# An adaLN transformer block on one core: the modulation is made with the conditions as TensorE's stationary side and turned back, and the condition is loaded and activated ahead of the biases

## The chip, the cores and the metric

The kernel runs on one core of a Trainium2 chip. The metric is device time in microseconds for one execution, the median of several. Five engines work side by side, each with its own queue in program order: TensorE (PE, with its weight loads shown apart as PEld), VectorE (DVE), ScalarE (ACT), GpSimd (POOL) and SyncE (SP), which here only issues DMAs. ScalarE issues some DMAs too, in line with its other instructions.

## The reference

Sixteen batches of 224 tokens of width 512, a condition vector of 512 per batch, and a context of 750 tokens per batch. Everything is float32.

```python
c_proj = jax.nn.silu(c) @ W_mod + b_mod
shift_a, scale_a, gate_a, shift_m, scale_m, gate_m = jnp.split(c_proj, 6, axis=-1)
x_norm = modulate(_ln(x), shift_a, scale_a)        # t * (1 + scale) + shift, per batch
q, k, v = split(x_norm @ W_qkv + b_qkv)            # 16 heads of 32
x = x + gate_a[:, None] * (attention(q, k, v) @ W_proj + b_proj)
x = x + cross_attention(_ln(x), _ln(context)) @ W_cproj + b_cproj
x_norm2 = modulate(_ln(x), shift_m, scale_m)
h = jax.nn.gelu(x_norm2 @ W_mlp1 + b_mlp1)
x = x + gate_m[:, None] * (h @ W_mlp2 + b_mlp2)
```

The change touches only how the first two lines are made. The condition is 16 x 512, W_mod is 512 x 3072. The six parts of 512 columns are numbered 0 to 5: shift, scale, gate of self-attention, then shift, scale, gate of the MLP.

## The kernel before

The kernel has three stages one after the other: self-attention in 8 pairs of batches (`p`), cross-attention in 16 batches, and the MLP in 7 groups of 512 tokens. `Ordered` makes every engine keep the order in which the program issues, so each engine's queue is as written.

The head (lines 248 to 274 and 589 to 608) loads the condition, the parts of W_mod and the first two batches; activates the condition (`c_act`), turns it so that its 512 features lie on partitions (`c_t`); turns all biases, which are loaded as rows of 128 (`brow`), to columns (`bcol`), and adds 1 to those of the scales; norms the first two batches (`norms[j].all()`: bn_stats on DVE, the rest on POOL); and calls `make_part(0)` and `make_part(1)`. Then `turn_x` turns the normed rows on PE, and DVE applies shift and scale while it evicts them to `xt`, from which q, k and v are projected.

A shift or scale is wanted as columns: `mod_t` holds, for each 128 features, one column per batch. `make_part` therefore takes 128 x 128 blocks of W_mod as the stationary side and the 16 columns of `c_t` as the moving one: 16 matmuls, each streaming 16 columns. In the profile one float32 matmul of this kind is two rows of PE. A gate (parts 2 and 5) is wanted as rows: there `c_t` is stationary (16 columns) and W_mod streams 512 columns, in 4 matmuls; the bias rows `bg` are added and the gate is written to DRAM, from where it is read back spread over the token rows.

Parts 0 and 1 are made in the head. The other four are placed in the first units of self-attention. A unit is one group of 4 heads in one batch; `plan[p, u, slot]` lists what else runs in the two slots of unit `u` of pair `p`. Part 2 is at (0, 1, 0), part 3 at (0, 1, 1), parts 4 and 5 at (0, 3, 0) and (0, 3, 1). The loads of W_mod go through two buffers, so a later part's load waits until PE has used the buffer. All small PE results pass through `ps_mm`, three PSUM banks in rotation, and a bank is free again when it has been evicted. One unit on PE is: scores, slot 0, the weights of the unit before (`weights_t`), the turn of the row maxima, slot 1, the values and sums of the unit before.

The DMAs of SP and ScalarE take turns on a small set of completion semaphores. A DMA can thus wait, at its issue, for an unrelated earlier one that used the same semaphore; this decides some of the waits at the head.

Of the kernel before, what the change touches and what calls it, by code (L numbers as in the profile page):

```python
# [8 lines left out]
F32 = mybir.dt.float32  # L9
BF16 = mybir.dt.bfloat16  # L10
AF = mybir.ActivationFunctionType
ALU = mybir.AluOpType
# [25 lines left out]
def kernel(  # L38
# [23 lines left out]
    nc = Ordered(tc)  # L62
    B, N, H = x.shape
    S = context.shape[1]
    MLP = w_mlp1.shape[1]
    P = 128
    NH = 16
    HD = H // NH
    KC = H // P
# [20 lines left out]
    SCALE = float(HD) ** -0.5  # L90
# [3 lines left out]
    const = ctx.enter_context(tc.tile_pool(name="const", bufs=1))  # L94
# [3 lines left out]
    ident = const.tile([P, P], F32, name="ident")  # L98
# [33 lines left out]
    o_mod, o_qkv = 0, 6 * KC  # L132
    o_qc = o_qkv + 3 * KC
    o_kvc = o_qc + KC
    o_mlp = o_kvc + 2 * KC
    nbias = o_mlp + NF
    brow = const.tile([nbias, P], F32, name="brow")
    for off, vec in ((o_mod, b_mod), (o_qkv, b_qkv), (o_qc, b_qc), (o_kvc, b_kvc), (o_mlp, b_mlp1)):
        rows = vec.shape[0] // P
        nc.scalar.dma_start(out=brow[off : off + rows, :], in_=vec.rearrange("(r p) -> r p", p=P))  # L140
    bcol = const.tile([P, nbias], F32, name="bcol")

    def bias_rows(pool, vec, rows, name):
# [21 lines left out]
    def load_w(pool, w, name, bufs=1):  # L165
        kc = w.shape[0] // P
        t = pool.tile([P, kc, w.shape[1]], F32, name=name, bufs=bufs)
        nc.sync.dma_start(out=t, in_=w.rearrange("(k p) n -> p k n", p=P))
        return t

    mm, turn = nc.tensor.matmul, nc.tensor.transpose
# [65 lines left out]
    mp = mod_pool.enter_context(tc.tile_pool(name="mod", bufs=2, side="right"))  # L237
    attention_psum = ExitStack()
    ps_s = attention_psum.enter_context(tc.tile_pool(name="at_s", bufs=1, space=PSUM))
    ps_mm = attention_psum.enter_context(tc.tile_pool(name="at_mm", bufs=3, space=PSUM))  # L240
    ps_o = attention_psum.enter_context(tc.tile_pool(name="at_o", bufs=1, space=PSUM))
    xs = {}
    w_part = {}

    def load_part(i):
        w_part[i] = load_w(mp, w_mod[:, i * H : (i + 1) * H], "w_mod", 2)

    c_in = mp.tile([B, H], F32, name="c_in", bufs=1)
# [3 lines left out]
        xs[b] = load_x(sa, tokens(x, b), 6)  # L252
    load_part(1)
    wq, wk, wv = (load_w(ws, w_qkv[:, i * H : (i + 1) * H], f"wqkv{i}") for i in range(3))
    bg = mp.tile([B, 2, H], F32, name="bg", bufs=1)
    for i in range(2):
        lo = (2 + 3 * i) * H
        nc.scalar.dma_start(out=bg[:, i, :], in_=b_mod[lo : lo + H].partition_broadcast(B))

    c_act = mp.tile([B, H], F32, name="c_act", bufs=1)  # L260
    nc.scalar.activation(c_act, c_in, AF.Silu)

    c_t = mp.tile([P, KC, B], F32, name="c_t", bufs=1)
    ps = ps_mm.tile([P, 512], F32, name="mm")
# [1 line left out]
        turn(ps[:, k * B : (k + 1) * B], c_act[:, k * P : (k + 1) * P], ident[:B, :B])  # L266
    nc.vector.tensor_copy(c_t.rearrange("p k b -> p (k b)"), ps[:, : KC * B])

    ps = ps_mm.tile([P, 512], F32, name="mm")
    turn(ps[:, :nbias], brow, ident[:nbias, :nbias])  # L270
    nc.vector.tensor_copy(bcol, ps[:, :nbias])
    for i in (1, 4):
        sl = bcol[:, o_mod + i * KC : o_mod + (i + 1) * KC]
        nc.vector.tensor_scalar(sl, sl, 1.0, None, ALU.add)

    bqc = const.tile([P, KC], F32, name="bqc")
    nc.vector.tensor_scalar(bqc, bcol[:, o_qc : o_qc + KC], SCALE, None, ALU.mult)

    def make_part(i):
        w = w_part[i]  # L280
        ps = ps_mm.tile([P, 512], F32, name="mm")
        if i % 3 == 2:
            for k in range(KC):
                mm(ps[:B, :H], c_t[:, k, :], w[:, k, :], start=(k == 0), stop=(k == KC - 1))
            g = mp.tile([B, H], F32, name="gates", bufs=1)
            nc.vector.tensor_tensor(g, ps[:B, :H], bg[:, i // 3, :], ALU.add)
            nc.sync.dma_start(out=gate_d[i // 3], in_=g)
        else:
            slot = (i // 3) * 2 + i % 3
            for m in range(KC):  # L290
                for k in range(KC):
                    mm(
                        ps[:, m * B : (m + 1) * B], w[:, k, m * P : (m + 1) * P], c_t[:, k, :],
                        start=(k == 0), stop=(k == KC - 1),
                    )
            for m in range(KC):
                nc.vector.tensor_scalar(
                    mod_t[:, slot * KC + m, :], ps[:, m * B : (m + 1) * B],
                    bcol[:, o_mod + i * KC + m : o_mod + i * KC + m + 1], None, ALU.add,
                )  # L300
# [99 lines left out]
    def whole(products):  # L400
        for _ in products:
            pass
# [32 lines left out]
    if True:  # L435
# [8 lines left out]
        def project_qk(p, m):  # L444
            ps = ps_mm.tile([P, 512], F32, name="mm")
            for k in range(KC):
                mm(
                    ps[:, :PN], (wq, wk)[m // KC][:, k, (m % KC) * P : (m % KC + 1) * P], xts[p][k],
                    start=(k == 0), stop=(k == KC - 1),
                )  # L450
                if k == 1:
                    yield
            t = sa.tile([P, PN], F32, name="qk", bufs=6)
            bm = bcol[:, o_qkv + m : o_qkv + m + 1]
            if m < KC:
                nc.vector.tensor_scalar(t, ps[:, :PN], bm, SCALE, ALU.add, ALU.mult)
            else:
                nc.scalar.activation(t, ps[:, :PN], AF.Identity, bias=bm)
            qk[p, m] = t
# [30 lines left out]
        def project(p, t):  # L490
            b, c = PB * p + t // TC, t % TC
            if c == 0:
                gate[b] = gate_rows(sa, 0, b * N, TP)
            ps = ps_mm.tile([P, 512], F32, name="mm")
            yield from project_heads(ps, at[p], wproj, t * TP)
            add_to_x(sa, ps[:TP, :H], xs[b][:, c, :], bproj, gate[b])
            if c == TC - 1:
                nc.sync.dma_start(out=x_self[b], in_=xs[b])
# [3 lines left out]
        def at_slot(p, u, slot, f):  # L502
            if p < NP:
                plan.setdefault((p, u, slot), []).append(f)

        for p in range(NP):
            if p < NP - 1:
                for g in range(1, KC):
                    at_slot(p, 2 * g - 2, 0, lambda p=p, g=g: whole(project_qk(p, g)))
                    at_slot(p, 2 * g - 2, 1, lambda p=p, g=g: whole(project_qk(p, KC + g)))  # L510
                for t in range(PT if p else 0):
                    at_slot(p, 1 + t // 2 * 2, t % 2, lambda p=p, t=t: whole(project(p - 1, t)))
            else:

                left = [(project_qk, p, m) for m in (1, KC + 1, 2, KC + 2)]
                left += [(project, p - 1, t) for t in range(2)]
                left += [(project_qk, p, m) for m in (3, KC + 3)]
                left += [(project, p - 1, t) for t in range(2, PT)]
                parts = [h for f, *args in left for h in halves(lambda f=f, args=args: f(*args))]
                for i, h in enumerate(parts):  # L520
                    at_slot(p, i // 3, i % 3 // 2, h)
            if p == 0:
                at_slot(p, 1, 0, lambda: make_part(2))
                at_slot(p, 1, 1, lambda: make_part(3))
                at_slot(p, 1, 1, lambda: load_part(4))
                at_slot(p, 1, 1, lambda: load_part(5))
                at_slot(p, 3, 0, lambda: make_part(4))
                at_slot(p, 3, 1, lambda: make_part(5))
                at_slot(p, 3, 1, load_cross)
            n = p + 1  # L530
            if n < NP:
                if n > 1:
                    at_slot(p, 0, 0, lambda n=n: fetch(n))
                at_slot(p, 1, 0, lambda n=n: norm_begin(n))
                for t in range(PT):
                    at_slot(
                        p, 1 + t // 2, t % 2, lambda n=n, t=t: norms[PB * n + t // TC].stats(t % TC)
                    )
                for j in range(PB):
                    at_slot(p, 1 + j, 1, lambda n=n, j=j: norms[PB * n + j].apply())  # L540
                for k in range(KC):
                    at_slot(p, 4, k // 2, lambda n=n, k=k: turn_x(n, k))
                for t in range(PT):
                    at_slot(p, 5 + t // 2, t % 2, lambda n=n, t=t: project_v(n, t))
                at_slot(p, 7, 0, lambda n=n: whole(project_qk(n, 0)))
                at_slot(p, 7, 1, lambda n=n: whole(project_qk(n, KC)))
# [42 lines left out]
        norm_begin(0)  # L589
        for j in range(PB):  # L590
            norms[j].all()
        make_part(0)
        make_part(1)
        load_part(2)
        load_part(3)
        fetch(1)
# [142 lines left out]
    class First:  # L739
# [22 lines left out]
        def part(self):  # L762
            return cw["mx"].tile([P, H], F32, name="mx")
# [39 lines left out]
    with tc.tile_pool(name="ca", bufs=2, reuse_waits="tile") as ca:  # L803
# [98 lines left out]
        for b in range(B):  # L902
            n = b + 1
            for g in range(KC):
                f, m = (b, g + 1) if g < KC - 1 else (n, 0)
# [399 lines left out]
```

## Time and profile before

| what | value |
| --- | --- |
| runs shown | 2964.05, 2967.8, 2962.16 us; median 2964.05 |
| profiled execution | 2967.63 us |
| its span, first to last instruction | 2965.8 us |
| what lies around the span | 1.83 us |
| mean granted TensorE clock | 0.989 |
| PE rows / busy | 19901 / 2877.7 us |
| first matmul | 9.97 us |
| first normed tile `xt` | 25.57 us |
| scores of unit 4 end | 98.9 us |

All times of the trace are microseconds from the start of the span. In a timeline row the first number is the start, the second how long the piece lasts (several merged instructions may be one piece), then engine, line, operation, out<-in, the shape, the count, and in brackets the idle time before it and what ended that. Nearly all instructions show line 28, the recording helper of `Ordered`, so they are told apart by tile names. A line of the windows gives the stretch, its length, busy time and count of PE, PEld, DVE, ACT and POOL, and last the granted clock, the DMA share and GB/s. A busy PE is not PE at its peak: ends of matmuls are modelled.

### The profile page before, as it was taken

Reading aid. Unit: us, or ns where it says so; the run is one execution under the profiler, and the core shown is the slowest. Engines: PE = TensorE matmul, PEld = TensorE weight load, DVE = VectorE, ACT = ScalarE, POOL = GpSimd, SP = SyncE. Lnnn points to the kernel's source line nnn. Section 1 sums busy time; section 2 is a strip of 40 time slices with the busy share of each in tenths; the row PEclk is TensorE's granted clock in tenths of the full one; section 3 lists DMA queues with packets and bytes.
Section 4 is the critical chain, followed back from the end, with each engine's and each line's share of the span. In section 5 each row is a group of like instructions: output and inputs, shape, how many; then the busy total and the mean of one; then the engine's idle time right before and its main releaser. Section 6 shows DMA issues by size and latency. Waiting matters only on the chain.

```text
span 2965.8 us, 47584 instructions
## 1 busy us (share of the span) xinstructions
PE 2877.7 (97%) x19901; PEld 1851.1 (62%) x19901; DVE 1843.2 (62%) x2624; ACT 1175.4 (40%) x1462; POOL 1289.0 (43%) x1636
## 2 busy tenths in 40 slices
PE   8999999999999999999999999999988999999999
PEld 5544444544455655555556556555655888888888
DVE  2556555566377777777777877877776633443343
ACT  1122121222356656656665666566553122112211
POOL 1022211122266766766767766667664510221021
PEclk9999999999999999999999999999999999999999
DMA  5111101100100101000011001010011211111110
GB/s 183 63 32 32 32 10 29 53 20 20 60 21 22 34 24 34 30 19 31 24 34 34 24 22 34 24 34 24 7 58 67 74 36 54 43 40 36 54 43 29
DMA packets 55387, 114.47 MB, mean 39 GB/s; under 512 B 4308, under 2 KB 4372, under 8 KB 55172
## 3 DMA queue, kind: packets, MB, share of 16 engines
q1 hardware_dynamic: 54560, 110.58, 11.6%
q8 instruction: 156, 2.56, 0.4%
q10 hardware_dynamic: 612, 0.85, 0.1%
q14 instruction: 59, 0.48, 0.1%
HBM read 89.33 MB, written 22.09 MB: 38 GB/s over the span
## 4 chain that ended last, share of the span: by engine, by line
PE 81%; DVE 7%; issue 4%; ACT 3%; POOL 3%; DMA 1%; SPq 0%; ACTq 0%; POOLq 0%; DVEq 0%
PE mm L28 46%; PE a L28 10%; PE sc L28 9%; PE o L28 9%; PE b L28 5%; ACT pt L28 3%; PE c L28 3%; DVE top L28 1%; POOL acc L28 1%; DVE rinv L28 1%; DVE stats L28 1%; DVE mc L28 1%; DVE m L28 1%; ACT kt L28 1%; POOL upd L28 0%
## 5 line engine op out<-in xcount | busy, mean ns | idle before, releaser
L28 POOL TENSOR_TENSOR acc<-acc,pt 125x448 f32<-125x448 f32 x512 | 585.1, 1143 | 40.2
L28 DVE TENSOR_TENSOR pt<-pt,o 125x896 f32<-125x896 f32 x384 | 394.3, 1082 | 92.1 <-PE o L28 87.0
L28 ACT COPY pt<-sc 125x1792 f32<-125x1792 f32 x192 | 317.5, 1654 | 223.3 <-DVE top L28 198.9
L28 DVE TENSOR_TENSOR top<-top,sc 125x896 f32<-125x896 f32 x320 | 346.6, 1083 | 40.7 <-PE sc L28 34.0
L28 POOL TENSOR_TENSOR upd<-upd,gate 112x512 f32<-112x512 f32 (+1 forms) x60 | 79.1, 1318 | 668.9 <-DVE upd L28 664.3
L28 PE MATMUL mm<-wkvc,cxt 128*125 128x512 f32 x768 | 354.4, 604 | 8.6 <-ACT kt L28 8.6
L28 PE MATMUL mm<-cxt,wkvc 128*128 128x375 f32 x1024 | 349.8, 484 | 2.4 <-ACT cxt L28 2.4
L28 ACT ACTIVATE pt<-pt 125x896 f32<-125x896 f32 x384 | 339.1, 955 | 12.6 <-DVE pt L28 11.9
L28 POOL TENSOR_TENSOR acc<-pt 125x448 f32<-125x448 f32 x128 | 146.6, 1146 | 380.3 <-ACT pt L28 380.3
L28 DVE RECIPROCAL rinv<-o 128x224 f32<-128x224 f32 x128 | 198.7, 1553 | 108.6 <-PE o L28 108.6
L28 PEld LDWEIGHTS mm<-cxt,wkvc 128*128 128x128 f32 x1024 | 190.1, 191 | 112.4 <-issue 12.8
L28 DVE TENSOR_REDUCE m<-sc 112x8 f32<-112x1792 f32 x64 | 129.7, 2026 | 209.4 <-PE sc L28 209.4
L28 ACT ACTIVATE pt<-sc 112x1792 f32<-112x1792 f32 x64 | 106.5, 1665 | 365.4 <-PE sc L28 365.4
L28 PEld LDWEIGHTS mm<-wkvc,cxt 128*125 128x125 f32 x768 | 136.5, 187 | 175.1 <-issue 153.5
L28 POOL TENSOR_TENSOR rstd<-mv,eps 112x2 f32<-112x2 f32 (+3 forms) x93 | 18.0, 194 | 475.7 <-DVE mv L28 475.7
L28 PE MATMUL sc<-qt,kt 32*125 32x224 f32 x3072 | 202.7, 378 | 12.9 <-ACT pt L28 12.3
L28 PE MATMUL mm<-xt,wqkv 128*128 128x448 f32 x512 | 209.6, 552 | 4.7 <-DVE xt L28 4.7
L28 PEld LDWEIGHTS sc<-qt,kt 32*125 32x125 f32 x3072 | 134.0, 184 | 92.9 <-issue 41.2
L28 ACT COPY mrow<-mm 128x896 bf16<-128x896 bf16 x64 | 58.0, 906 | 309.5 <-PE mm L28 309.5
L28 PE MATMUL o<-pt,vt 125*32 125x224 f32 x3072 | 158.5, 354 | 0.0
L28 PEld LDWEIGHTS mm<-xt,wqkv 128*128 128x128 f32 x512 | 92.5, 191 | 86.8 <-issue 81.0
L28 ACT COPY mx<-a 128x512 f32<-128x512 f32 x26 | 15.2, 586 | 325.1 <-POOL upd L28 306.3
(193 smaller groups left out, 4815.1 us busy)
## 6 DMA issues: line engine op xcount, KB each, us to landing
cx<-in_ctx_dram SPq DMA_DIRECT2D x96, 250.0 KB
x<-in_x_dram SPq DMA_DIRECT2D x16, 448.0 KB
x_self<-x SPq DMA_DIRECT2D x16, 448.0 KB
x<-x_self SPq DMA_DIRECT2D x16, 448.0 KB
x_cross<-x SPq DMA_DIRECT2D x16, 448.0 KB
mx<-x_cross SPq DMA_DIRECT2D x28, 256.0 KB
w<-in_L_xcond_W_mlp_dram SPq DMA_DIRECT2D x7, 1024.0 KB
xr<-x_cross SPq DMA_DIRECT2D x28, 256.0 KB
```

What stands on the lines that cost most here:

```text
L28: return lambda *args, **kw: self.tc.keep_in_program_order(f(*args, **kw))
```

## The change

The shift and scale parts are made in the form that the gates had. `make_part` is split in two: `part_rows(i)` has `c_t` as stationary side, streams W_mod in 4 matmuls of 512 columns and, for a shift or scale, copies the 16 x 512 result to SBUF on ScalarE; `finish_part(i, ...)` turns that in four 128-column pieces on PE and adds the bias columns on DVE as before. The gates do both at once.

In the head, parts 0 and 1 are made as rows before the biases are turned (`make_columns`), and are finished after that. In self-attention, part 3's finish is one slot later, in unit 2; part 4's is in the slot of part 5, behind it.

On ScalarE's queue the condition's load is now the first DMA, the activation is the first computation, and the loads of `brow` and `bg` follow it. DVE takes the first bn_stats ahead of the bias columns.

```diff
-    for off, vec in ((o_mod, b_mod), (o_qkv, b_qkv), (o_qc, b_qc), (o_kvc, b_kvc), (o_mlp, b_mlp1)):
-        rows = vec.shape[0] // P
-        nc.scalar.dma_start(out=brow[off : off + rows, :], in_=vec.rearrange("(r p) -> r p", p=P))
...
     wq, wk, wv = (load_w(ws, w_qkv[:, i * H : (i + 1) * H], f"wqkv{i}") for i in range(3))
+    c_act = mp.tile([B, H], F32, name="c_act", bufs=1)
+    nc.scalar.activation(c_act, c_in, AF.Silu)
+    for off, vec in ((o_mod, b_mod), (o_qkv, b_qkv), (o_qc, b_qc), (o_kvc, b_kvc), (o_mlp, b_mlp1)):
+        rows = vec.shape[0] // P
+        nc.scalar.dma_start(out=brow[off : off + rows, :], in_=vec.rearrange("(r p) -> r p", p=P))
     bg = mp.tile([B, 2, H], F32, name="bg", bufs=1)
...
-    c_act = mp.tile([B, H], F32, name="c_act", bufs=1)
-    nc.scalar.activation(c_act, c_in, AF.Silu)
...
+    def make_columns():
+        ps = ps_mm.tile([P, 512], F32, name="mm")
+        turn(ps[:, :nbias], brow, ident[:nbias, :nbias])
+        nc.vector.tensor_copy(bcol, ps[:, :nbias])
...
+    def part_rows(i):
+
+        ps = ps_mm.tile([P, 512], F32, name="mm")
+        for k in range(KC):
+            mm(ps[:B, :H], c_t[:, k, :], w_part[i][:, k, :], start=(k == 0), stop=(k == KC - 1))
+        if i % 3 < 2:
+            r = mp.tile([B, H], F32, name="part", bufs=2)
+            nc.scalar.copy(r, ps[:B, :H])
+            return r
+        return ps
+
+    def finish_part(i, ps):
         if i % 3 == 2:
-            for k in range(KC):
-                mm(ps[:B, :H], c_t[:, k, :], w[:, k, :], start=(k == 0), stop=(k == KC - 1))
...
         else:
             slot = (i // 3) * 2 + i % 3
+            rows, ps = ps, ps_mm.tile([P, 512], F32, name="mm")
             for m in range(KC):
-                for k in range(KC):
-                    mm(
-                        ps[:, m * B : (m + 1) * B], w[:, k, m * P : (m + 1) * P], c_t[:, k, :],
-                        start=(k == 0), stop=(k == KC - 1),
-                    )
+                turn(ps[:, m * B : (m + 1) * B], rows[:, m * P : (m + 1) * P], ident[:B, :B])
...
-                at_slot(p, 1, 0, lambda: make_part(2))
-                at_slot(p, 1, 1, lambda: make_part(3))
+                at_slot(p, 1, 0, lambda: part(2))
+                at_slot(p, 1, 1, lambda: part(3))
                 at_slot(p, 1, 1, lambda: load_part(4))
                 at_slot(p, 1, 1, lambda: load_part(5))
-                at_slot(p, 3, 0, lambda: make_part(4))
-                at_slot(p, 3, 1, lambda: make_part(5))
+                at_slot(p, 2, 0, lambda: finish_part(3, made[3]))
+                at_slot(p, 3, 0, lambda: part(4))
+                at_slot(p, 3, 1, lambda: part(5))
+                at_slot(p, 3, 1, lambda: finish_part(4, made[4]))
                 at_slot(p, 3, 1, load_cross)
...
-        make_part(0)
-        make_part(1)
+        rows = [part_rows(i) for i in range(2)]
+        make_columns()
+        for i in range(2):
+            finish_part(i, rows[i])
```

More of the change, by code (lines that the diff above doesn't have):

```diff
@@ L267 @@
     nc.vector.tensor_copy(c_t.rearrange("p k b -> p (k b)"), ps[:, : KC * B])
[L269 to L274, printed above, removed]
     bqc = const.tile([P, KC], F32, name="bqc")
-    nc.vector.tensor_scalar(bqc, bcol[:, o_qc : o_qc + KC], SCALE, None, ALU.mult)
-    def make_part(i):
-        w = w_part[i]
+    def make_columns():
         ps = ps_mm.tile([P, 512], F32, name="mm")
+        turn(ps[:, :nbias], brow, ident[:nbias, :nbias])
+        nc.vector.tensor_copy(bcol, ps[:, :nbias])
+        for i in (1, 4):
+            sl = bcol[:, o_mod + i * KC : o_mod + (i + 1) * KC]
+            nc.vector.tensor_scalar(sl, sl, 1.0, None, ALU.add)
+        nc.vector.tensor_scalar(bqc, bcol[:, o_qc : o_qc + KC], SCALE, None, ALU.mult)
+    def part_rows(i):
[8 more added lines that the diff above has]
+    def finish_part(i, ps):
         if i % 3 == 2:
-            for k in range(KC):
-                mm(ps[:B, :H], c_t[:, k, :], w[:, k, :], start=(k == 0), stop=(k == KC - 1))
             g = mp.tile([B, H], F32, name="gates", bufs=1)
@@ L522, with part @@
             if p == 0:
-                at_slot(p, 1, 0, lambda: make_part(2))
-                at_slot(p, 1, 1, lambda: make_part(3))
+                made = {}
+                def part(i):
+                    made[i] = part_rows(i)
+                    if i % 3 == 2:
+                        finish_part(i, made[i])
+                at_slot(p, 1, 0, lambda: part(2))
+                at_slot(p, 1, 1, lambda: part(3))
                 at_slot(p, 1, 1, lambda: load_part(4))
                 at_slot(p, 1, 1, lambda: load_part(5))
-                at_slot(p, 3, 0, lambda: make_part(4))
-                at_slot(p, 3, 1, lambda: make_part(5))
+                at_slot(p, 2, 0, lambda: finish_part(3, made[3]))
+                at_slot(p, 3, 0, lambda: part(4))
+                at_slot(p, 3, 1, lambda: part(5))
+                at_slot(p, 3, 1, lambda: finish_part(4, made[4]))
                 at_slot(p, 3, 1, load_cross)
```

## The prediction

> **What bounds the kernel now.** I read the page first, then the chain of waits, then the timeline of the first 100 us, then the windows of the stretches in which the modulation is made. The page says that TensorE is the bound:
>
> ```profile
> PE 2877.7 (97%) x19901; PEld 1851.1 (62%) x19901; DVE 1843.2 (62%) x2624; ACT 1175.4 (40%) x1462; POOL 1289.0 (43%) x1636
> PE 81%; DVE 7%; issue 4%; ACT 3%; POOL 3%; DMA 1%; SPq 0%; ACTq 0%; POOLq 0%; DVEq 0%
> ```
>
> So an edit counts where it shortens PE's own queue or lets it start earlier. The modulation stands in two places: at the head, where PE has nothing else, and in the first units of self-attention, where PE has no gap. The chain at the head:
>
> ```profile
> 2.92 6.26 DMA c_in<-in_cond_dram
> 10.87 41.12 PE mm L28 x136
> ```
>
> The conditions take 6.26 us to land at 9.18, and PE starts after that. The timeline shows what follows:
>
> ```profile
> 3.40 3.34 ACTq L28 DMA_DIRECT2D bg<-in_L_xcond_b_mod_dram  x2
> 6.77 1.28 ACT L28 ACT_TABLE_LOAD   x1 [6.77 <-DMA w_mod<-in_L_xcond_W_mod_dram]
> 9.20 0.63 ACT L28 ACTIVATE c_act<-c_in 16x512 f32<-16x512 f32 x1 [1.15 <-DMA c_in<-in_cond_dram]
> 10.87 13.84 PE L28 MATMUL mm<-c_t,w_mod 128*128 128x16 f32 x64
> 24.74 0.66 DVE L28 TENSOR_SCALAR mod_t<-mm,bcol 128x16 f32<-128x16 f32 x4 [6.17 <-PE mm L28]
> 25.57 3.44 DVE L28 TENSOR_SCALAR xt<-mm,mod_t 128x224 f32<-128x224 f32 x8 [0.17 <-PE mm L28]
> 27.56 7.26 PE L28 MATMUL mm<-xt,wqkv 128*128 128x448 f32 x16
> ...
> 60.27 3.61 PE L28 MATMUL mm<-w_mod,c_t 128*16 128x512 f32 x8
> 65.00 4.92 PE L28 MATMUL mm<-c_t,w_mod 128*128 128x16 f32 x32
> 69.85 1.72 PE L28 MATMUL o<-pt,v 112*32 112x224 f32 x16
> ```
>
> Shift and scale of the first half (64 PE rows) hold PE for 13.84 us; the first normed tile xt waits for them. A gate part, already in the new form, takes 8 rows and 3.61 us; a shift part in the old form 32 rows and 4.92 us. The windows (last three columns: granted clock, DMA share, GB/s) show a second cost:
>
> ```profile
> 66.00:67.00 1.00, 1.00 (x12) 1.00 (x11) 0.00 (x0) 0.70 (x1) 0.00 (x0) 1.00 0.02 2
> 67.00:68.00 1.00, 1.00 (x8) 1.00 (x8) 0.00 (x0) 0.00 (x0) 0.00 (x0) 0.62 0.77 141
> 73.00:74.00 1.00, 1.00 (x16) 0.91 (x16) 0.00 (x0) 0.00 (x0) 0.98 (x2) 0.50 1.03 403
> 74.00:75.00 1.00, 1.00 (x14) 0.52 (x7) 0.40 (x1) 0.00 (x0) 0.77 (x1) 0.96 1.02 373
> 87.00:88.00 1.00, 1.00 (x10) 1.00 (x10) 0.90 (x5) 0.00 (x0) 0.00 (x0) 0.86 0.00 0
> 94.00:95.00 1.00, 1.00 (x3) 0.15 (x2) 0.00 (x0) 0.00 (x0) 0.00 (x0) 0.72 0.00 0
> ```
>
> About 2.3 us into the 16-wide products of part 3 the clock falls to 0.50 and returns at 74.05; part 4 does the same from 87.7 to 94.3. In between everything on PE takes double: the 16 value products 1.72 us, against 0.96 in the next unit. At the head the column reads 1.00 throughout, but the durations do not agree: loads of 128 columns take 333 to 338 ns there and 186 warm, and 448-wide products go by at 0.74 us until 29.7 and at 0.375 after. I take the head as cold up to 29.7.
>
> **Head, step by step.** (1) c_in takes the place of the first bias rows on ScalarE's queue (issue at 0.72). In the built order bg's first issue waits for that copy, and it went out at 3.40, so c_in should land by about 3.4 to 4; at worst as now, 5.8 us after issue, 7.2. The table load is done by then. From c_act to the start of the products is 1.66 us (9.20 to 10.86): c_t at 5.1 to 5.7 (worst 8.9). (2) Then w_mod part 0 decides. It landed at about 6.4, since the second bg issue waited for it. On SP's queue the built order has x1 no longer waiting for a bias copy (5.0 us now), and w_mod part 1 waiting for c_in only; the stream of 385 GB/s then runs without the hole at 7 to 8 us. [...] (3) Two parts are 16 rows: 0.88 us each cold, 0.44 warm (3.53 us by 8, from 60.27 to 63.80). Such rows do warm the clock: part 5 began cold at 91.12 and had it back at 94.3, after 3.2 us. So 3.6 rows cold and 12.4 warm: 6.4 + 3.2 + 5.5 = 15.1. Bounds: 6.6 us cold (as long as both dips) 16.7; cold throughout 20.5. (4) Behind them PE turns brow (0.36), then part 0; ScalarE copies part 1 (0.6, near the 0.59 of v); PE turns it (0.58 for four in the c_act row); DVE makes bcol and two times four mod_t (0.66 each): mod_t ends at about 17.4. [...] (5) xt begins at 17.5 against 25.57: 8.0 us gained; 3 to 10 by the bounds.
>
> The bias copies: brow and bg now wait behind the activation, and bias rows of b_mlp1 also for part 0, so they are issued from 4.1 to 6.8 into a full stream. By the nearest row, c_in's 5.8 us from issue to landing, brow is complete at 12.5, before PE asks at 15.1: no cost. [...] I take the row. [...]
>
> Does the gain grow because the wide products now meet a warm PE? The trace loses its clock 2.3 us into thin work (65.0 to 67.3), and 4.4 us of turns lie between the rows and the first 448-wide product at 19.5. [...]
>
> **First units.** Part 3: from 65.00 to 74.46 in the old form. In the new one 3.53, plus values and sums 1.65 (82.03 to 83.68), plus scores 0.95: 6.13 instead of 9.46, 3.3 gained. Part 4 to the end of part 5: 84.63 to 96.42, 11.8 now. New: 3.53, weights 1.09 (77.66 to 78.75), max turn 0.1, part 5 3.53, four turns 0.5: 8.75, 3.0 gained. Part 3's turns one unit later: 0.5 lost. They also take one of three mm banks, so the K projection in unit 2 now waits for DVE's evict of Q in the bank before last. DVE has m, four splits, reciprocal, at and the evict in front (74.61 to 80.03, 5.6 us after scores end); PE would come there after 3.2 + 0.5 + 1.1 + 0.1 = 4.8: 0.8 lost, with values behind it. ScalarE's two part copies stand beside exp at 1.67 us per unit of some 10: cover enough; without it, 0.6 each. The four mod_t move behind Q's evict or the gates, no later than PE's need in unit 4. SP now sends the gate read ahead of w_mod part 5; that read waits for the gate write of 64.6, landed before part 3's buffer is free: 0. First units: 3.3 + 3.0 - 0.5 - 0.8 = 5.0; bounds 2.5 (a dip returns, as each is worth 2 to 3) to 6.5.
>
> From unit 4 the engines' orders are the same as before, PE-bound, so the shift lasts. Sum 8.0 + 5.0 = 13 us against the profiled execution (span 2965.8, 2967.63 in all, 3.6 above the median): 2954.6 there, 2951 against the median 2964.05.
>
> **Rivals.** *The head is freed and then waits again*: rows stay cold or brow and w_mod come late, head 3, first units 3: 6 to 8, 2957. For it: the 13.84 us are cold now. Against: the 3.2 us recovery at 91.12. [...] *Slower: the biases come last.* PE's queue is in order and brow's turn stands ahead of every xn turn. Each us that brow lands after 15.1 is a us lost; from 28 on nothing is left of 13, and from 34 it is slower by 0.2%. It would take small copies served only when SP's stream ebbs (some 30 us with parts 2, 3, x and wproj behind it) and more contention; 37 would give 2973. For it: five small copies took up to 9.18 in a lighter stream. Against: they landed while w_mod part 1 was streaming.
>
> **Numbers.** Forecast 0.62 (2951, own range 2946 to 2956), waits again 0.22 (2957), dips remain 0.09 (2962), slower 0.07 (2973). The range 2945 to 2960 leaves out 0.2. About 0.2% (6 us) is what a measurement can tell from no change. Faster 0.82, same 0.11, slower 0.07.
>
> **What would show it.** c_act before 5; 8 rows of w_mod,c_t from about 6.5, twice; xt near 17.5; granted clock 1.00 through parts 3 and 4; a short PE wait on DVE ahead of the K projection of unit 2; unit 4 some 13 us earlier. It is wrong if PE waits for brow, if parts wait for w_mod, or if the clock dips in spite of wide rows.

## The result and the profile after

The changed kernel took 2955.24 us (median of 6 runs, 2954.09 to 2955.72), the kernel before 2965.36 us beside it (6 runs): a ratio of 0.9966, interval 0.9953 to 0.9979. Over all comparisons below, 117 runs of before have a mean of 2964.6 us and 14 of the changed one 2955.5: 9.2 us less. The forecast of 2951 held in its direction, in its steps and within its range of 2946 to 2956; the gain is 9 to 10 us, not 13.

The profiled execution took 2954.09 us, 13.5 less than the one profiled before. So the pair of profiles shows the 13 us that were forecast, and the medians do not. Both have to be explained.

First the engine row of the page, to hold against the one of before:

```profile
PE 2866.0 (97%) x19821; PEld 1828.5 (62%) x19821; DVE 1845.5 (63%) x2624; ACT 1177.6 (40%) x1466; POOL 1286.2 (44%) x1636
```

PE has 80 rows less (four parts from 32 rows to 8, plus 4 turns each) and 11.7 us less busy time; ScalarE has the four new copies. Next the timeline of the head (start, length, engine, operation, idle time before it):

```profile
0.72 0.45 ACTq L28 DMA_DIRECT2D c_in<-in_cond_dram  x1
3.84 0.63 ACT L28 ACTIVATE c_act<-c_in 16x512 f32<-16x512 f32 x1 [1.35 <-DMA c_in<-in_cond_dram]
6.36 5.47 PE L28 MATMUL mm<-w_mod,c_t 128*16 128x512 f32 x8 [1.17 <-DMA w_mod<-in_L_xcond_W_mod_dram]
12.71 3.61 PE L28 MATMUL mm<-w_mod,c_t 128*16 128x512 f32 x8 [0.87 <-DMA w_mod<-in_L_xcond_W_mod_dram]
16.24 0.28 PE L28 MATMUL mm<-ident,brow 64*128 64x64 f32 x1
16.45 0.94 PE L28 MATMUL mm<-ident,part 16*128 16x16 f32 x8
18.17 3.44 DVE L28 TENSOR_SCALAR xt<-mm,mod_t 128x224 f32<-128x224 f32 x8
20.03 6.25 PE L28 MATMUL mm<-xt,wqkv 128*128 128x448 f32 x16 [0.22 <-PE mm L28]
```

The activation is 5.4 us earlier (9.20 before), xt 7.4 us (25.57) and the first q product 7.5 (27.56). The first eight rows take 5.47 us against the 3.61 of the second eight: their weight loads start 0.85 us apart up to 9.73 and 0.43 apart from 10.38 on, so PE starts at half speed ("cold") and comes to full speed ("warm") while they run. The biases' turn stands directly behind the rows and waits for nothing. The q products then end 1.0 us sooner after their start than before (6.25 for 16 and no stretch at half speed, against 7.26). PE's weight loads show it, first before, then after:

```profile
28.34 0.34 PEld L28 LDWEIGHTS mm<-xt,wqkv 128*128 128x128 f32 x1 [0.41 <-issue]
29.77 0.19 PEld L28 LDWEIGHTS mm<-xt,wqkv 128*128 128x128 f32 x1 [0.35 <-issue]
```

```profile
20.48 0.19 PEld L28 LDWEIGHTS mm<-xt,wqkv 128*128 128x128 f32 x1 [0.19 <-issue]
```

The first loads of before take 0.34 us, a cold PE, and only from 29.77 on 0.19; those of after take 0.19 from the start. Then the first units after, with the Q projection of unit 4 of before at the end, and the windows from 40 to 100 us, before first and after below it:

```profile
56.56 3.18 PE L28 MATMUL mm<-w_mod,c_t 128*16 128x512 f32 x7
65.77 0.29 PE L28 MATMUL mm<-ident,part 16*128 16x16 f32 x2
68.19 3.27 PE L28 MATMUL mm<-xt,wqkv 128*128 128x448 f32 x8 [0.81 <-DVE qk L28]
74.00 3.61 PE L28 MATMUL mm<-w_mod,c_t 128*16 128x512 f32 x8
85.32 3.27 PE L28 MATMUL mm<-xt,wqkv 128*128 128x448 f32 x8
...
98.82 2.52 PE L28 MATMUL mm<-xt,wqkv 128*128 128x448 f32 x6
```

```profile
40.00:100.00 60.00, 60.00 (x387) 31.88 (x386) 24.65 (x52) 9.30 (x9) 5.91 (x12) 0.89 0.14 45
```

```profile
40.00:100.00 60.00, 58.09 (x431) 27.13 (x430) 33.85 (x69) 11.58 (x11) 5.88 (x12) 1.00 0.33 115
```

The clock is 1.00 through parts 3 and 4 (0.89 before, with a dip of the clock behind each of the two parts). In unit 2 the K projection waits 0.81 us for DVE's evict of Q, the wait that the prediction put at 0.8. PE reaches the Q projection of unit 4 at 85.32 against 98.82. From there to the end of the span it is 2867.0 us in both profiles (2952.3 - 85.32 and 2965.8 - 98.82). So in this pair all 13.5 us arise in the first 100: 7.5 in the head, 1.0 in the warm q products, 5.0 in the units. That the rest is equal to the tenth is luck: over three profiles of before it is 2867.0, 2863.3 and 2866.4, over two of the changed kernel 2867.0 and 2868.3.

### The profile page after: what moved, and what is told of

Same layout as the page of the kernel before. It is cut to its first block, busy times and chain, and to the rows that moved or that the text cites. A ratio compares the mean times of both kernels' runs of the same rounds, so it can differ in the third digit from the quotient of the medians.

```text
span 2952.3 us, 47429 instructions
## 1 busy us (share of the span) xinstructions
PE 2866.0 (97%) x19821; PEld 1828.5 (62%) x19821; DVE 1845.5 (63%) x2624; ACT 1177.6 (40%) x1466; POOL 1286.2 (44%) x1636
```

## The experiments

Three durations separate head, units and rest in each profile: the start of xt, the time from the first q product to the Q projection of unit 4 ("q to unit 4"), and the rest. In the first pair q to unit 4 is 71.3 us before and 65.3 after. "By means" below is against the runs of before that were taken with the run in question.

**e1: the head alone.** From the changed kernel, `make_part` of before is put back in the units.

```diff
-                at_slot(p, 1, 1, lambda: part(3))
+                at_slot(p, 1, 1, lambda: make_part(3))
...
-                at_slot(p, 2, 0, lambda: finish_part(3, made[3]))
-                at_slot(p, 3, 0, lambda: part(4))
+                at_slot(p, 3, 0, lambda: make_part(4))
```

> The changed head with the old products of parts 3 and 4 in the first units. Main theory (two separate gains, neither given back later): first xt at 18.2, first q product at 20.0, the granted clock falls to 0.50 behind parts 3 and 4 as in the kernel before, time 8.5 us below before. Rival (the head's gain is swallowed by waits of the units): xt as early, but unit 4 no more than 4 us earlier and the time within 4 us of before.

2958.29 us (median of 10), ratio 0.9981 (0.9971 to 0.9991); by means 6.3 us below before, where 8.5 were expected. xt begins at 19.5, not near 18: its two parts start at 7.39 and 14.03, each behind a wait for w_mod (1.66 and 0.43 us). Both clock dips are there (0.91 over 40 to 100), the second shorter than in the first profile of before; q to unit 4 is 68.5. The head is worth about 6.

**e2 and e11: the units alone.** From the kernel before, with the new `part_rows` and `finish_part` in the units only; e11 is the same kernel once more.

```diff
-                at_slot(p, 1, 1, lambda: make_part(3))
+                at_slot(p, 1, 1, lambda: part(3))
...
-                at_slot(p, 3, 0, lambda: make_part(4))
+                at_slot(p, 2, 0, lambda: finish_part(3, made[3]))
+                at_slot(p, 3, 0, lambda: part(4))
```

> The old head with parts 3 and 4 made as rows in the first units. Main theory: xt at 25.6 as before, granted clock 1.00 through units 1 to 4, scores of unit 4 end 5 us earlier than before (at 93.9), time 5 us below before. Rival (the dips of the clock are not due to the thin products): the clock falls to 0.50 here too and the time is within 2 us of before.

> e2_units_only once more, for a second profile: its first profile lost 5.4 us in the units, but its ten runs have a mean only 2.1 us below those of before. Theory (the dips that are gone in the units come back in part elsewhere, where PE waits for other engines, by where the clock's window falls): no dip in units 1 to 3 again; a run near 2962 to 2963 shows 2 to 4 us more than the first profile in the stretches after unit 4, with more clock lost between self- and cross-attention or before the MLP. Rival (the units themselves differ from run to run): a dip or a longer head in the first 100 us.

e2: 2963.0 us, ratio 0.9997 (0.9987 to 1.0006). e11: 2963.03 us, ratio 0.9989 (0.998 to 0.9998). By means e2 is 2.3 us below before and e11 2.6; over both, 21 runs against all of before, it is 2.1. Five were expected. Yet both profiles have a clock of 1.00 from 40 to 100, and q to unit 4 is 65.9 and 66.2, some 5 us better than the 71.3 of the first profile. So the units do what was foreseen, and the time shows half of it. Either something is given back later, or the first profile of before is not typical. The windows from 700 to 850 us, where self-attention ends and cross-attention begins, of e2 and then of e11:

```profile
700.00:850.00 150.00, 136.04 (x883) 74.58 (x885) 73.79 (x108) 53.92 (x64) 51.51 (x64) 0.97 0.15 49
```

```profile
700.00:850.00 150.00, 136.03 (x840) 73.46 (x839) 73.16 (x106) 51.72 (x62) 48.65 (x61) 0.93 0.15 45
```

The column before the DMA share is the granted clock: the same kernel has 0.97 here in one execution and 0.93 in the other. Length times what is missing to 1.00 is the loss in us of full speed: 5 and 10. Summed microsecond by microsecond over the fourteen profiles of this case, it lies between 3.4 and 10.2 us, in no order by kernel (before: 8.5, 3.4, 6.8; changed: 8.5, 5.1). The sums are all close to multiples of 1.7 us, what 3.4 us at half clock lose; the two dips of e1 last 6.8 and 3.4 us. So the clock is lost here in pieces of one length, and what differs between executions is how many. The changes also lie on a raster: in the first profile of before the clock falls or returns at 67.25, 74.07, 87.73 and 94.55, distances of two, four and two times 3.41 us. The expectations speak of the clock's window; what the traces show of one is this raster.

**e7, e12: the kernel before again; e8: the changed kernel again.** No edit.

> The kernel before, unchanged, for a second profile. Its runs lie in two groups, near 2962 and near 2967; the changed kernel's lie within 2 us. Theory (the thin products meet the clock's window in different places): the profile of a run in the lower group shows one dip less, or shorter ones, in units 1 to 3 or elsewhere. Rival: the same dips, and the difference lies spread over the whole span or around it.

> The kernel before for a third profile. Theory: both dips behind parts 3 and 4 again, but their lengths vary with the clock's window (6.7 and 6.6 us in the first profile; 7 and 3.4 us are possible, as in e1_head_only), and so does the rest of the span; a short dip gives less than 5 us to gain in the units. Rival: always two dips of 6.7 us.

> The changed kernel, unchanged, for a second profile. Theory (the q product of the head was warm by where the clock's window fell): the first q product comes near 20.0 again, but may take 0.74 us per row up to some 2 us. Rival (the wide rows of parts 0 and 1 keep the clock through the turns): 0.375 us per row from the start again. Units 1 to 4 without a dip either way.

Before: 2963.98 and 2963.47 us (ratios 1.0003 and 0.9999); changed: 2955.95 us, ratio 0.9971 (0.9961 to 0.9981). e7 has both dips, as the first profile, although one fewer was expected of a run near 2964. e12 does not have both. Its timeline and, below it, windows of the two places:

```profile
64.68 3.70 PE L28 MATMUL mm<-c_t,w_mod 128*128 128x16 f32 x32
68.31 0.96 PE L28 MATMUL o<-pt,v 112*32 112x224 f32 x16
...
81.09 4.71 PE L28 MATMUL mm<-c_t,w_mod 128*128 128x16 f32 x32
```

```profile
67.00:68.00 1.00, 1.00 (x11) 1.00 (x11) 0.00 (x0) 0.00 (x0) 0.00 (x0) 1.00 1.01 385
...
84.00:85.00 1.00, 1.00 (x6) 1.00 (x6) 1.00 (x2) 0.00 (x0) 0.00 (x0) 0.50 0.00 0
```

Part 3 goes through at full clock in 3.70 us (4.92 in the first profile) and the values behind it take 0.96; only part 4 dips. q to unit 4 is 67.7 instead of 71.3. The kernel before thus has one dip or two, by execution; the one that the prediction was worked from had two, and lost 8.5 us of clock at 700 to 850 besides. The executions profiled in e7 and e12 lost 5.1 us less over both places (10.2 against 15.3) and took 3.6 and 4.1 us less (2964.06 and 2963.49 against 2967.63).

e8 repeats the changed kernel's units (q to unit 4 65.3, no dip, warm q products), but its head is slower by 1.4:

```profile
7.71 5.71 PE L28 MATMUL mm<-w_mod,c_t 128*16 128x512 f32 x8 [1.79 <-DMA w_mod<-in_L_xcond_W_mod_dram]
```

**e3: the new order, the old form.** From the kernel before: the condition first and the biases behind the activation, the columns made after parts 0 and 1, these in the thin form; units as before.

```diff
+    c_act = mp.tile([B, H], F32, name="c_act", bufs=1)
+    nc.scalar.activation(c_act, c_in, AF.Silu)
+    for off, vec in ((o_mod, b_mod), (o_qkv, b_qkv), (o_qc, b_qc), (o_kvc, b_kvc), (o_mlp, b_mlp1)):
...
+        make_columns()
```

> ScalarE's new order (conditions first, biases behind), columns of the biases after the products, but parts 0 and 1 in the old form, and the old units. Main theory (order and form share the head): products start at 6.4 when w_mod part 0 is there, take 13.8 us as before with PE cold, end at 20.2, xt at 22.4: 3.2 us below before. Rival (the load order carries the head alone): xt near 18.2 and 7 to 8 us below before.

2965.52 us, ratio 1.0008 (0.9999 to 1.0018): nothing gained.

```profile
8.53 13.81 PE L28 MATMUL mm<-c_t,w_mod 128*128 128x16 f32 x64 [2.37 <-DMA w_mod<-in_L_xcond_W_mod_dram]
24.28 3.43 DVE L28 TENSOR_SCALAR xt<-mm,mod_t 128x224 f32<-128x224 f32 x8
```

The activation is 4.4 us earlier than in before, but part 0 of w_mod is now what PE waits for (2.37 us), so the products start 2.3 earlier; and with the columns behind them xt follows 1.9 us after the last product instead of 0.9. xt at 24.3 is 1.3 us earlier, where 3.2 were expected; the dips stay.

**e4: the form, the old order.** From the changed kernel with ScalarE's queue as before.

```diff
+    for off, vec in ((o_mod, b_mod), (o_qkv, b_qkv), (o_qc, b_qc), (o_kvc, b_kvc), (o_mlp, b_mlp1)):
+        rows = vec.shape[0] // P
+        nc.scalar.dma_start(out=brow[off : off + rows, :], in_=vec.rearrange("(r p) -> r p", p=P))
...
-    c_act = mp.tile([B, H], F32, name="c_act", bufs=1)
-    nc.scalar.activation(c_act, c_in, AF.Silu)
```

> The whole change except ScalarE's order: biases are loaded first, conditions after them, activation behind bg. Main theory: c_t at 10.9 as before, the 16 rows of the two parts end 9.1 us later at 20, xt at 21.9 (3.7 gained), q product warm (1 gained), units 5 gained: 9.7 us below before in all. Rival (the order alone carries the head): xt at 24 or later and 5 to 6 us below before.

2958.09 us, ratio 0.9979 (0.9969 to 0.9988); 7.1 us below before by means, where 9.7 were expected.

```profile
11.09 9.36 PE L28 MATMUL mm<-w_mod,c_t 128*16 128x512 f32 x16 [0.32 <-DVE c_t L28]
22.31 3.43 DVE L28 TENSOR_SCALAR xt<-mm,mod_t 128x224 f32<-128x224 f32 x8
```

With the old order w_mod is there in time (the rows wait for c_t, not for it): all sixteen rows run as one piece of 9.36 us, where the 64 thin ones took 13.84, and xt is 3.3 earlier than in the first profile of before. The form carries most of the gain. The order adds some 2 us to it (2957.7 against 2955.5 by means), less than the 5 us by which the activation comes earlier, as PE then waits for w_mod (1.17 to 1.99 us ahead of part 0 in the changed kernel, e1, e6, e8 and e9).

**e5: the clock without the new form.** From the kernel before: parts 3 and 4 keep all their thin products, cut into stretches of 16 rows with other work between.

```diff
-                at_slot(p, 1, 1, lambda: make_part(3))
+                at_slot(p, 1, 1, lambda: part_half(3, 0))
+                at_slot(p, 2, 0, lambda: part_half(3, 1))
...
-                at_slot(p, 3, 0, lambda: make_part(4))
+                at_slot(p, 2, 1, lambda: part_half(4, 0))
+                at_slot(p, 3, 0, lambda: part_half(4, 1))
```

> The kernel before, with the thin products of parts 3 and 4 cut in two stretches of 16 rows each (part 3 in units 1 and 2, part 4 in units 2 and 3): as many thin rows as before, but never more than about 2.1 us of them in a run, and the load of part 5 one slot later. Main theory (a long run of thin products lets the clock fall): no dip to 0.50 in units 1 to 3, scores of unit 4 end 4 to 5 us earlier than before. Rival (what counts is the number of rows, or a mean over more than a unit): the dips stay, unit 4 within 1 us of before.

2960.14 us, ratio 0.9984 (0.9975 to 0.9994); 4.2 us below before by means.

```profile
63.88 1.92 PE L28 MATMUL mm<-c_t,w_mod 128*128 128x16 f32 x16
65.73 0.96 PE L28 MATMUL o<-pt,v 112*32 112x224 f32 x16
71.45 1.85 PE L28 MATMUL mm<-c_t,w_mod 128*128 128x16 f32 x16
81.89 1.96 PE L28 MATMUL mm<-c_t,w_mod 128*128 128x16 f32 x16
```

```profile
40.00:100.00 60.00, 58.65 (x426) 32.48 (x425) 30.67 (x64) 10.97 (x10) 5.88 (x12) 1.00 0.26 88
```

No dip: the clock is 1.00 from 40 to 100, and the values behind the first stretch take 0.96. So here the number of thin rows does not bring the dips: as many of them, in stretches of at most 1.96 us with other work between, leave the clock at 1.00, while the uncut run of 32 went with a dip in nine of ten cases (two runs in each profile of before, e1, e3, e7 and e12). And q to unit 4 is 64.5, no worse than with the new form. By the times the cut thin products gain more than the new form in the units did (4.2 us against 2.3 and 2.6), although they save no row; the intervals overlap.

**e6: the wait in unit 2 taken away, the columns between the parts.**

```diff
-                at_slot(p, 2, 0, lambda: finish_part(3, made[3]))
+                at_slot(p, 2, 1, lambda: finish_part(3, made[3]))
...
-        rows = [part_rows(i) for i in range(2)]
+        rows = [part_rows(0)]
         make_columns()
+        rows.append(part_rows(1))
```

> The changed kernel with two moves: part 3 is finished one slot later, behind the K projection of unit 2; and the biases are turned between the rows of part 0 and part 1. The first tells whether the bank of the added turns makes PE wait for the eviction of Q: by that theory the wait of 0.8 us ahead of K in unit 2 is gone and unit 4 comes 0.8 us earlier against its first q product; otherwise the wait stays. The second shows when the bias rows are there: PE asks for them at 11.8. [...]

2955.43 us, ratio 0.997 (0.9958 to 0.9981).

```profile
7.32 6.02 PE L28 MATMUL mm<-w_mod,c_t 128*16 128x512 f32 x8 [1.76 <-DMA w_mod<-in_L_xcond_W_mod_dram]
13.27 0.14 PEld L28 LDWEIGHTS mm<-ident,brow 64*128 64x128 f32 x1 [0.85 <-DMA brow<-in_L_xcond_b_mlp_dram]
13.27 0.28 PE L28 MATMUL mm<-ident,brow 64*128 64x64 f32 x1
...
67.94 3.23 PE L28 MATMUL mm<-xt,wqkv 128*128 128x448 f32 x8
```

K in unit 2 no longer waits, and q to unit 4 is 64.4 instead of 65.3: the 0.8 of the prediction is confirmed by its removal. And the turn of the biases at 13.27 stands directly behind the eight rows: the last bias row had landed by then. Its weight load names that row as what came last, but with the same 0.85 us that it shows in the changed kernel, where it waits for nothing; how long before 13.27 the row landed, the trace does not tell.

**e10: are the loads behind part 0 what holds it up?** From the changed kernel, x of the second batch, part 1 of w_mod and the q, k, v weights are issued from ScalarE after activation and biases.

```diff
-    for b in range(PB):
-        xs[b] = load_x(sa, tokens(x, b), 6)
-    load_part(1)
-    wq, wk, wv = (load_w(ws, w_qkv[:, i * H : (i + 1) * H], f"wqkv{i}") for i in range(3))
+    xs[0] = load_x(sa, tokens(x, 0), 6)
...
+    nc.scalar.dma_start(out=xs[1], in_=tokens(x, 1))
```

> The changed kernel with the loads of the second x, w_mod part 1 and the three qkv weights issued by ScalarE behind the activation and the biases, so that only w_mod part 0 and the first x are on the DMA engines until about 5 us. Theory (in the changed kernel part 0 comes late, 6.4 to 8.5 us, because loads issued right behind it share the DMA engines; before they were held until 6.6): part 0's rows start at 6.6 or earlier. The rest of the head then waits for part 1, which is issued after part 0 has landed, so the first xt is no earlier than in the changed kernel (19 to 20). Rival (part 0's landing varies by itself): rows start anywhere from 6.4 to 8.5 again.

2957.22 us (8 runs, 2952.74 to 2962.63), ratio 0.9975 (0.9965 to 0.9985). Part 0's rows start at 6.74, run on into those of part 1 without a wait, and xt begins at 18.4, earlier than the 19 to 20 that were expected. 6.74 lies at the early end of the profiles with the new order, 6.36 to 8.53 (mean 7.5 of six), but one profile inside the spread, of the fastest of the eight runs, decides nothing, and the time is no better. What makes part 0 land late stays open.

**e9: the new head with the split thin units**, which the above points to: the changed kernel with the units of e5.

```diff
-                at_slot(p, 1, 1, lambda: part(3))
+                at_slot(p, 1, 1, lambda: part_half(3, 0))
+                at_slot(p, 2, 0, lambda: part_half(3, 1))
...
-                at_slot(p, 3, 0, lambda: part(4))
+                at_slot(p, 2, 1, lambda: part_half(4, 0))
+                at_slot(p, 3, 0, lambda: part_half(4, 1))
```

> The changed head with the cut thin products in the units (part 3 in units 1 and 2, part 4 in units 2 and 3, as in e5_split_thin), so that nothing is turned or copied in the units. Main theory (in the units only the length of a thin run mattered, and the rows' turns and their bank cost more than the rows saved): no dip, no wait ahead of K in unit 2, from the first q product to the end of scores of unit 4 63.6 us (64.5 of the split kernel less 0.9 of cold q products) against 65.3 of the changed kernel, and a time 1.7 us below the changed kernel, near 2953.7. Rival (thin runs cool the clock more easily beside the new head): a dip returns and the time is 2957 or above.

2954.58 us (6 runs), ratio 0.9967 (0.9955 to 0.998) against before. No dip, no wait of K, q to unit 4 64.0 (65.3 in the changed kernel). Its mean is 1.2 us below that of the changed kernel, where 1.7 were expected; these runs cannot tell that from nothing.

## Why the prediction was right, and where its sum was off

**Bound and place.** That PE's own queue sets the time, and that a shift in the first 100 us lasts to the end, is borne out: the head alone (e1) brings its gain to the end. The rest, from unit 4 to the end of the span, took 2867.0 us in both of the first pair; over all profiles it scatters from 2863.3 to 2868.3.

**The condition (step 1).** c_act at 3.84, in the forecast 3.4 to 4; 4.07 to 4.80 in the other profiles of this order, a little late. It is not what PE waits for.

**Part 0 (step 2) is the term of the head that was mis-sized.** 6.4 was read from one execution of before; the first profile after has 6.36, but the six with the new order have 7.5 in the mean. The sum lets the rows of part 1 follow those of part 0 without a wait, and none of the five profiles with the new form in the new order shows that: in the first PE waited 0.87 us for w_mod there and began them at 12.71, in e1, e6, e8 and e9 it waited 0.30 to 0.66 and began them at 13.85 to 14.62. So the rows ended at 16.3 in the best case (15.1 forecast) and near 17.6 in e1 and e8; xt begins at 18.2 there and at 19.3 in the mean of e1, e6, e8, e9 and the first profile. Old heads begin it at 25.3 (mean of before, e7, e12, e2, e11, e5). That is 6.0 us where 8.0 were booked, inside the bounds of 3 to 10.

**The clock at the head.** By the cold stretch of 3.2 us that was taken from part 5 (its clock is back at 94.55, after 3.4) the first eight rows would take 5.1 us; they took 5.47, and 5.71 to 6.25 in e1, e6, e8 and e9. So PE was cold for 3.7 to 5.3 us there, an estimate: twice what these pieces take over 3.61. The sum has nothing for the q products, and that was wrong: all seven profiles with the new form in the head have them warm (6.25 us), the seven with thin products there take 6.78 to 7.26, 0.8 more in the mean. The row (clock lost after 2.3 us of thin work) did not foresee that: the first profile has 3.7 us of turns, gaps included, between the last row and the first q product, and the 16 q products behind them took 6.25 us. Why, no run here tells.

**The biases.** By the row of c_in (5.8 us from issue to landing) they were to be complete at 12.5, before PE would ask at 15.1. e6 bears that out as far as it reaches: there by 13.27. No cost, as booked.

**The units.** The working agrees with the pair of profiles: 5.0 forecast, 5.0 found; 0.8 for K's wait, 0.81 found (its four terms add up to 4.9, not 4.8, so the last tenth is luck). But it compares with an execution of two full dips. Over five profiles of the thin units, q to unit 4 is 71.3, 71.0, 67.7, 71.1 and 68.5 (the last with a warm q product); over five of the new units (after, e8, e4, e2, e11), 65.3 to 66.2. With an old head the gain at unit 4 is on average 4.2 (mean 70.3 of before, e7, e12, e3 against 66.0 of e2, e11). The time shows some 2.3; the intervals of e2 and e11 reach to 3.9 and 5.9. Whether what is missing is given back behind unit 4 or is scatter is not settled: the stretch from unit 4 to the end takes 2865.8 us in the mean of the five profiles of the long thin products and 2866.8 in that of the seven of the new form, and the clock loss at 700 to 850 alone goes from 3.4 to 10.2 us whatever the kernel.

**The sum.** 6.0 and 0.8 for the head (e1: 6.3 by the times) and some 2.3 for the units (e2, e11) make 9.1; the change measured 9.2. Where 13 were forecast, 2 were lost at the two parts of w_mod, 0.8 won at the q products, and some 2.7 of the units are missing: part of it stood for dips that not every execution of before has (5.0 in the pair, 4.2 on average), the rest is open. That the pair of profiles gave 13.5 is luck: it set the execution of before with the most lost clock of three against the earliest head of all profiles, and the two terms that were off in the head (w_mod late, q products warm) offset each other in part.

**The rivals.** "The head is freed and then waits again" (2957) named the term that was short, w_mod coming late, and its time of 2957 is nearer to the result of 2955.2 than the 2951 of the forecast. That the dips remain (2962) fell: in none of the seven profiles with the new form in the units is the clock below 1.00 there. e5 narrows it: a short thin run does as well. "The biases come last" fell with e6.

## What to carry to other kernels

Price a thin matmul by its rows and by the clock behind it: here 64 thin rows of 13.8 us became 16 wide ones of 9.4, and with a run of 32 the clock was at 0.50 for up to 6.8 us; in the units, cutting such a run in two did as well as the new form. Before a load's consumer is brought forward, look at the next load: here the order alone gave nothing (ratio 1.0008 in e3), as PE then waited 2.37 us for part 0 of w_mod. And where a clock dip is part of the sum, take more than one profile of the kernel before: the dips came and went by execution, and the pair of profiles showed 5.0 us in the units where the average was 4.2.

## What the runs showed of the hardware that was not expected

- The same 32 thin products (128x16) at the same place (part 3) were followed by a clock of 0.50 in four of the five profiles that have them, and not in e12, which ran them in 3.70 us at 1.00. In e5 and e9 the stretches of 16 (up to 1.96 us) never were.
- The clock was lost in pieces of about 3.4 us at 0.50: all sums of lost clock at 700 to 850 are near multiples of 1.7 us.
- After wide rows PE stayed warm through 3.7 us of small turns; after 13.8 us of thin products it was cold. At the head the granted clock reads 1.00 in both cases: the durations (0.34 against 0.19 us for one weight load) tell it.
- A 1 MB load issued first, at 0.72 us, let PE start anywhere between 6.36 and 8.53 us in six profiles with the same order of issue around it.
